# A graph layer's front part: B alone beside the comparisons, A + x behind the counts, and the first 24 rows by searches for the eight largest

## The chip, the cores and the metric

The kernel runs on one core of one Trainium2 chip. The metric is device time of one execution in microseconds (us). The engines are PE (TensorE), DVE (VectorE), ACT (ScalarE), POOL (GpSimd) and SP (SyncE, which issues most DMAs here). Each engine runs its instructions in the order in which the program gives them; PE's clock is granted between half and full speed.

## The reference

x has 6250 rows of 128 numbers; src and dst are 206,250 edges, sorted by dst, each node with a loop of its own.

```python
h = jnp.maximum(_layernorm(x, axis=-1), 0.0)
x_i = h[dst]
x_j = h[src]
feat = jnp.concatenate([x_i, x_j - x_i], axis=-1)
msg = feat @ W.T + b
out = jax.ops.segment_max(msg, dst, num_segments=x.shape[0])
x = x + jnp.where(jnp.isfinite(out), out, 0.0)
```

With W = [W1 W2], msg = A[dst] + B[src], where A = h (W1 - W2)^T + b and B = h W2^T. A[dst] is the same for all edges of one dst, so the output is x + A + the maximum of B[src] over a node's edges.

## The kernel before, in words

Each of 128 partitions takes a window of 1792 edges (WIN) that covers its 49 nodes. The stages, in order of time:

1. **Front (0 to 25.6 us).** The windows are found and gathered (src into swin, dst into pk), masks and tables are made, and the statistics of the first tenth of x.
2. **Comparisons (25.6 to 88).** For 41 lags, `shift` (L530, DVE) compares each edge's node with the one so many places ahead of it, and PE counts the matches into PSUM (`dup`, L519): an edge whose (dst, src block) already had an edge is not handled by the matmuls and goes on the list. Between the lags stand the *linear steps*, three for each k of 25 pairs of 125 rows: `turn` (transposes of h, L421, copy hT L422), `product` (bias L430, two 256-column products L433, copies of B: Bp L437 and a staging copy L438) and `remainder` (negI x Bp L446, copies L448 and L449). They are issued by `ln(n)`; 16 k's are done here, the rest later. B goes to HBM as Bt, A as XA (L455, on SP), and POOL adds x to XA in HBM by five accumulating DMAs (`add_x`, L441).
3. **List (88 to 155).** The sign of the counts (L591, ACT), a running sum over it (L610, the scan) that says how far each kept edge moves, and then 11 compaction passes (`pass_`, L633 and L634, DVE), of 1, 2, 4 ... places. After pass 4, `early` (L643 to L656) finds the first 24 entries of each list, and the first three groups of gathers are issued. PE meanwhile transposes the windows (`turned`, L666) and receives `tick`s: a small memset on DVE (L504) that a matmul waits for (L505), and eight matmuls whose result is not used (`keep_on`, L499). Behind the passes come the list's indices (ridx), the run ends, several checks whose sums go into badc, rows of Sel (`make_sel`, L256), and Sel's last two rows by DMA (L741, SP).
4. **Main loop (155 to 700).** 13 tiles x 25 pairs: one-hot matmuls (L903), ACT (L904), two products with Bp (L981), maximum into acc on DVE (L985, L987). Beside it goes the *stream* of 420 rows of listed edges: POOL gathers row k of all partitions (`gather`, L87) from Bt into the ring X, which holds six groups of eight rows; DVE takes a running maximum (L157, `stream_step`); SP writes each finished group to M (L164). A group's place is gathered into again once its write to M is over. `more_rows` fixes at which pair which gather and which step stands.
5. **End (700 to 767).** The 49 R gathers fetch each node's last row from M (L87, R<-M), then maximum, + XA, and the output.

The tiles of stages 2 and 3 lie in pools that are given back before stage 4. OHQ, the first tile of stage 4 that DVE sets (L885), lies in their memory.

X serves twice: until the linear steps have read x, its columns hold x (`xs`). acc, big and T are also used as temporary memory in the front part.

Of the kernel before, what the change touches and what calls it, by code (L numbers as in the profile page):

```python
# [8 lines left out]
F32 = mybir.dt.float32  # L9
F32R = mybir.dt.float32r  # L10
F16 = mybir.dt.float16
# [42 lines left out]
def gnn_kernel(tc, x, src, dst, W, b, out):  # L54
# [17 lines left out]
    EP = 5  # L72
    EW = 3 * U
    SETS = (WIN - EW - (1 << EP)) // (2 << EP) + 1
    assert EW + (1 << EP) <= 2 << EP and 16 < SETS <= 32 and WIN % (2 << EP) == 0
# [17 lines left out]
    with ExitStack() as ctx:  # L93
# [13 lines left out]
        with ExitStack() as body:  # L107
# [58 lines left out]
            with ExitStack() as pre:  # L166
# [45 lines left out]
                wmask = pool.tile([P, Q], F16, name="wmask")  # L212
# [8 lines left out]
                spare = acc[:1, 4 * GQ * C:]  # L221
# [38 lines left out]
                make_sel(0, 30)  # L260
                warm = pool.tile([P, 1], F32, name="warm")
# [57 lines left out]
                hs = [pool.tile([L, 2, C], F32, name=f"hs{i}") for i in range(2)]  # L319
                hT = [pool.tile([P, 2, P], F32, name=f"hT{i}") for i in range(2)]  # L320
# [22 lines left out]
                iota(pads, [[2, OV]], 0, 0)  # L343
# [27 lines left out]

                fl = pool.tile([P, 2 * NBLK], F32, name="fl")
                fin_ = big[:, :2 * C]
# [32 lines left out]
                bs = spare[:, 512:512 + 3 * P - 1]  # L406
# [4 lines left out]
                stage = acc[:L, :4 * GQ * C].rearrange("l (g q c) -> l g q c", g=4, c=C)  # L411

                def scaled(k):
                    for j in range(2):
                        q = 2 * k + j
                        A_.activation(hs[k % 2][:, j], xs[:, q], AF.Relu, scale=rstd[:, q:q + 1], bias=nmr[:, q:q + 1])  # L416

                def turn(k):
                    pt = ps_t.tile([P, 2, P], F32, name="pt")
                    for j in range(2):  # L420
                        T_.transpose(pt[:, j, :L], hs[k % 2][:, j], ident[:L, :L])  # L421
                    A_.copy(hT[k % 2][:, :, :L], pt[:, :, :L])  # L422

                def where(k):
                    g, o = divmod(2 * k, GQ)
                    return g % 2, o

                def product(k):
                    pm = steps[k]["pm"] = ps_m.tile([P, 2, 2 * C], F32, name="pm")
                    T_.matmul(pm[:L, :, C:], bsel, brow[:, C:].rearrange("k (o c) -> k o c", o=1).to_broadcast([P, 2, C]),  # L430
                              start=True, stop=False, skip_group_check=True)
                    for j in range(2):
                        T_.matmul(pm[:L, j], hT[k % 2][:, j, :L], wT, start=False, stop=j == 1, skip_group_check=True)  # L433
                    if k + 1 < NP_:
                        scaled(k + 1)
                    g, o = where(k)
                    A_.copy(Bp[:L, 0, 2 * k:2 * k + 2], pm[:L, :, :C])  # L437
                    A_.copy(stage[:, g, o:o + 2], pm[:L, :, :C])  # L438

                def add_x(q0):  # L440
                    G_.dma_start(out=XA_l[:, q0:q0 + GQ], in_=x_l[:, q0:q0 + GQ], accum_op=ALU.add)  # L441

                def remainder(k):
                    pm = steps[k].pop("pm")
                    g, o = where(k)
# [3 lines left out]
                    A_.copy(Bp[:L, 1, 2 * k:2 * k + 2], pm[:L, :, :C])  # L449
                    q0 = 2 * k - o  # L450
                    o0 = GQ - 4 if q0 + GQ == Q and o + 2 == GQ else 0
                    if o + 2 == GQ or q0 + GQ == Q and o + 2 == GQ - 4:
                        for to, j in ((Bt_l, g), (XA_l, 2 + g)):
                            for p0, p1 in PARTS:
                                S_.dma_start(to[p0:p1, q0 + o0:q0 + o + 2], stage[p0:p1, j, o0:o + 2])  # L455
                        if q0 + GQ < Q:
                            add_x(q0)

                micro = [lambda: turn(0)]
                for k in range(NP_):  # L460
                    micro.append(lambda k=k: product(k))
                    if k + 1 < NP_:
                        micro.append(lambda k=k: turn(k + 1))
                    micro.append(lambda k=k: remainder(k))

                def ln(n):
                    for _ in range(min(n, len(micro))):
                        micro.pop(0)()

# [9 lines left out]
                A_.activation(s16, sq, AF.Identity, bias=nthr)  # L479
                V.tensor_scalar(l16, sq, 1.0 / Q, (1 - Q) * 0.5 / Q, op0=ALU.mult, op1=ALU.add)  # L480
# [64 lines left out]
                def mine():  # L545
                    V.tensor_tensor(own, dlc, s16, ALU.is_equal)

                    def mm():
                        for c0 in range(0, WIN, 512):
# [9 lines left out]
                among[15] += [lambda: V.scalar_tensor_tensor(dwin, dlc, float(1 << DB), big, op0=ALU.mult, op1=ALU.add)]  # L559
                among[4] += [sel_rows]  # L560
                among[7] += [lambda: A_.activation(big, sq, AF.Copy, scale=float(1 << PB))]
# [7 lines left out]
                for i in range(SH):  # L569
                    among[i].append(lambda i=i: ln(2 if i % 5 == 4 else 1))  # L570
# [5 lines left out]
                flush(0)  # L576

# [8 lines left out]
                val = s16.bitcast(BF16)  # L586
                less = junk[0]
                spread_begin()
# [4 lines left out]
                make_sel(30, 40)  # L593
                finite(w_sb, 2 * C, P, 18)
                for v, op, o in ((VMAX, ALU.is_lt, badc[:L, 16:17]), (-VMAX, ALU.is_gt, badc[:L, 17:18])):
                    V.tensor_scalar(fin_[:L, :Q], mv[:, :, 1], v, None, op0=op, op1=ALU.add, accum_out=o)
                    V.tensor_scalar(o, o, -1.0, float(Q), op0=ALU.mult, op1=ALU.add)

# [10 lines left out]
                V.tensor_copy(u[:, :1], offs[:, :1])  # L609
                V.tensor_tensor_scan(u[:, 1:1 + WIN], sgn[:, :WIN], ones[:, :1].to_broadcast([P, WIN]), offs[:, :1],  # L610
                                     op0=ALU.add, op1=ALU.add)
                V.tensor_scalar(offs[:, 1:], offs[:, :1], -1.0, 2.0 * OV, op0=ALU.mult, op1=ALU.add)
                V.tensor_scalar(pk[:, :OV], pads, offs[:, 1:], 0.0, op0=ALU.subtract, op1=ALU.max)
                ln(2)
                p = ps_m.tile([P, 512], F32, name="pm")
                T_.matmul(p[:P - 1, :1], ident[:, 1:], offs[:, :1], start=True, stop=True)
                V.tensor_scalar(rlim[:P - 1], p[:P - 1, :1], -0.5, float(OV), op0=ALU.mult, op1=ALU.add)
                del p
                V.tensor_scalar_mul(over_, offs[:, 1:], 0.5)
                ln(6)  # L620
# [16 lines left out]

                def early():

                    s2 = 2 << EP  # L640
                    blocks = pk[:, OV:].rearrange("p (m r) -> p m r", r=s2)
                    F, FM = (swin[:, j * 32 * EW:(j + 1) * 32 * EW].rearrange("p (m w) -> p m w", w=EW) for j in range(2))
                    V.memset(mend_i, 0)  # L643
                    gather(mend, M[:P, :], mend_i[:, 0:1])
                    V.tensor_scalar(F[:, :SETS], blocks[:, :SETS, :EW], 0, None, op0=ALU.bitwise_or)
                    src_ = blocks[:, :SETS, s2 // 2:s2 // 2 + EW]
                    V.tensor_scalar(FM[:, :SETS], src_, 2 << EP, None, op0=ALU.bitwise_and)
                    V.copy_predicated(F[:, :SETS], FM[:, :SETS], src_)
                    d = 1
                    while d < SETS:  # L650
                        n = len(range(0, SETS - d, 2 * d))
                        f, m = (t.rearrange("p (a b) w -> p a b w", b=2 * d) for t in (F, FM))
                        V.tensor_scalar(m[:, :n, 0], f[:, :n, d], 4 * d << EP, None, op0=ALU.bitwise_and)
                        V.copy_predicated(f[:, :n, 0], m[:, :n, 0], f[:, :n, d])
                        d *= 2
                    V.tensor_scalar(ridx[:, :EW], F[:, 0], PB, (1 << DB - PB) - 1, op0=ALU.logical_shift_right,  # L656
                                    op1=ALU.bitwise_and)
                    for _ in range(EW // U):
                        gather_group()
                    V.scalar_tensor_tensor(val, dup, 0.0, vm, op0=ALU.is_equal, op1=ALU.mult)  # L660
# [21 lines left out]
                for i in range(EP):  # L682
                    rest[i].append(lambda i=i: ln(4 if i < EP - 1 else len(micro)))
# [6 lines left out]
                for i in (5, 6, 7, 8, 9, 10):  # L690
                    rest[i].append(lambda: tick(8))
# [5 lines left out]
                for i in range(11):  # L697
                    if i == EP:
                        early()
# [3 lines left out]
                add_x(Q - GQ)  # L703
# [8 lines left out]
                moved = u[:, :OV]  # L712
# [7 lines left out]
                for _ in range(GB - EW // U):  # L720
                    gather_group()
                sdl = u[:, OV:GR + OV]
# [16 lines left out]
                make_sel(40, Q)  # L739
# [8 lines left out]
                found()  # L748
                apart()
                finite(bsrc[:1], C, 1, 20)  # L750
# [347 lines left out]
```

## Time and profile before

| what | value |
|---|---|
| time, median of 3 runs (lowest, highest) | 769.29 us (769.13, 771.18) |
| the profiled execution's own time, and its span | 769.23 us, 767.5 us |
| mean granted clock of PE | 0.948 |
| busy: PE, DVE, ACT, POOL | 634.3, 721.8, 481.6, 505.3 us |
| X gathers on POOL | 420, 440.6 us |
| DVE idle in 700 to 768, for X gathers and R gathers | 6.8 us, 5.2 us |

A row of the timeline has the start, the duration, engine, line and operation, then what it writes and reads; in brackets stands the engine's idle time before it, and what ended it. PE's matmuls overlap in its pipe, so their cost is read from one start to the next. A POOL row of a gather is the writing of its descriptors; the transfer follows.

### The profile page before, as it was taken

To read this page: it belongs to the slowest core of one execution; us is meant where nothing else is said; L and a number is where in the kernel's file an instruction comes from. 1 tells how busy PE (TensorE), PEld (TensorE's weight loads), DVE (VectorE), ACT (ScalarE), POOL (GpSimd) and SP (SyncE) were. 2 spreads that over 40 slices of the span, in tenths; PEclk is the share of its full clock that TensorE was granted. 3 is DMA by queue.
4 is the path that set the end of the run, shared out by engine and by line. 5 is a ranking of instruction groups with operands and counts; after the bars stand their busy time and mean duration, and the time that the engine had idled before them with its cause. 6 is when DMAs were issued, how large, how long until landed. Compare 5 with 4: busy or idle time off the path is not lost.

```text
span 767.5 us, 11957 instructions
## 1 busy us (share of the span) xinstructions
PE 634.3 (83%) x3636; PEld 462.9 (60%) x3643; DVE 721.8 (94%) x1306; ACT 481.6 (63%) x1034; POOL 505.3 (66%) x522
## 2 busy tenths in 40 slices
PE   0699873568999898899989899999989899997871
PEld 0356542456667676666757667766757576775660
DVE  8999899979899999999999999999999999998584
ACT  3476681235789999565666767666666667676420
POOL 4000005877777777777777777777777777777774
PEclk9999996859999999999999999999999999999695
DMA  6533542143143433334333343334333343433494
GB/s 196 135 80 97 126 124 62 49 107 107 53 116 104 119 104 86 111 104 116 108 111 91 97 116 107 115 107 116 102 91 107 103 116 104 114 107 106 134 235 149
DMA packets 83699, 85.05 MB, mean 111 GB/s; under 512 B 9996, under 2 KB 71554, under 8 KB 83372
## 3 DMA queue, kind: packets, MB, share of 16 engines
q1 hardware_dynamic: 66951, 47.36, 21.7%
q0 software_dynamic: 16080, 35.93, 17.5%
q10 hardware_dynamic: 596, 0.92, 0.4%
q8 instruction: 30, 0.49, 0.3%
q14 instruction: 42, 0.34, 0.1%
HBM read 46.76 MB, written 40.47 MB: 114 GB/s over the span
## 4 chain that ended last, share of the span: by engine, by line
DVE 29%; PE 21%; issue 15%; DMA 5%; ACT 4%; POOL 2%; DVEq 0%; POOLq 0%
DVE acc L987 18%; PE ps L981 12%; DVE X L157 7%; PE z L903 5%; PE pv L835 4%; DMA X<-Bt,ridx 3%; ACT oh L904 2%; DMA R<-M,last_e 2%; ACT counted L994 2%; DVE OHQ L798 2%; POOL R L87 1%; POOL X L87 1%; DVE OHD L802 1%; DVE R L1019 1%; DVE acc L985 1%
## 5 line engine op out<-in xcount | busy, mean ns | idle before, releaser
L87 POOL DMA_INDIRECT X<-Bt,ridx x420 | 440.6, 1049 | 132.1 <-issue 40.2
L904 ACT ACTIVATE oh<-z 126x490 fp32r<-126x490 f32 (+1 forms) x650 | 340.4, 586 | 165.9 <-PE z L903 164.4
L981 PE MATMUL ps<-oh,Bp 126*128 126x490 f32 (+1 forms) x1300 | 393.3, 425 | 41.3 <-DVE acc L987 40.2
L987 DVE TENSOR_TENSOR acc<-acc,ps 128x980 f32<-128x980 f32 (+1 forms) x312 | 358.8, 1150 | 10.9 <-PE ps L981 8.1
L981 PEld LDWEIGHTS ps<-oh,Bp 126*128 126x128 f32 x1300 | 239.9, 193 | 137.6 <-DVE acc L987 92.3
L903 PE MATMUL z<-Vb,Sel 128*126 128x490 f16 (+1 forms) x650 | 196.1, 377 | 12.2 <-ACT oh L904 9.3
L157 DVE SCALAR_TENSOR_TENSOR X<-X,slim 128x128 f32<-128x128 f32 x419 | 143.5, 342 | 7.6 <-DMA X<-Bt,ridx 3.6
L903 PEld LDWEIGHTS <-Sel 128*126 128x126 f16 x650 | 87.0, 142 | 32.2 <-issue 3.9
L835 PEld LDWEIGHTS <-OHQ 128*128 128x128 bf16 x910 | 62.6, 162 | 16.3 <-issue 15.4
L835 PE MATMUL pv<-OHD,OHQ 128*128 128x28 bf16 (+1 forms) x896 | 67.2, 228 | 3.2 <-DVE OHD L805 3.1
L441 POOL DMA_DIRECT2D XA<-in_x x5 | 4.5, 902 | 89.6 <-DMA XA<-acc 89.6
L798 DVE TENSOR_TENSOR OHQ<-T,IQ 128x1092 bf16<-128x1092 bf16 (+5 forms) x104 | 61.4, 598 | 0.0
L87 POOL DMA_INDIRECT R<-M,last_e x49 | 49.6, 1012 | 16.4 <-issue 11.6
L994 ACT ACTIVATE counted<-lane_dl,nbias 128x556 bf16<-128x556 int32 x50 | 42.7, 853 | 0.1
L519 PE MATMUL dup<-T,identb 128*128 128x512 bf16 (+1 forms) x164 | 39.3, 364 | 3.7 <-DVE T L530 3.5
L433 PE MATMUL pm<-wT,hT 128*125 128x256 f32 x100 | 26.8, 392 | 0.3 <-ACT hT L422 0.3
L519 PEld LDWEIGHTS <-identb 128*128 128x128 bf16 x168 | 15.9, 101 | 17.2 <-issue 5.6
L634 DVE COPY_PREDICATED pk<-big,pk 128x1927 int32<-128x1927 int32 (+12 forms) x13 | 22.9, 1761 | 0.4
L416 ACT ACTIVATE hs<-X,nmr,rstd 125x128 f32<-125x128 f32 x50 | 22.1, 498 | 1.7 <-DVE nmr L314 1.7
L530 DVE TENSOR_TENSOR T<-KA,KB 128x1792 bf16<-128x1792 int16 x21 | 21.6, 1082 | 1.0 <-PE dup L519 1.0
L530 DVE TENSOR_TENSOR T<-KA 128x1792 bf16<-128x1792 int16 x20 | 20.8, 1077 | 0.1
L421 PE MATMUL pt<-ident,hs 125*128 125x125 f32 x50 | 12.6, 303 | 10.0 <-ACT hs L416 9.0
(271 smaller groups left out, 448.3 us busy)
## 6 DMA issues: line engine op xcount, KB each, us to landing
M<-X SPq DMA_DIRECT2D x52, 512.0 KB
X<-Bt,ridx POOLq DMA_INDIRECT x420
XA<-in_x POOLq DMA_DIRECT2D x5, 625.0 KB
ownb<-Bt SPq DMA_DIRECT2D x12, 245.0 KB
X<-in_x SPq DMA_DIRECT2D x5, 560.0 KB
Bt<-acc SPq DMA_DIRECT2D x4, 560.0 KB
XA<-acc SPq DMA_DIRECT2D x4, 560.0 KB
out_x<-R SPq DMA_DIRECT2D x8, 224.0 KB
```

The lines of the kernel that those rows point to most:

```text
L87: G_.indirect_dma_start(out=o, out_offset=None, in_=table, in_offset=bass.IndirectOffsetOnAxis(ap=idx, axis=0))
L157: V.scalar_tensor_tensor(G[:, j], state["prev"], slim[:, k:k + 1], G[:, j], op0=ALU.min, op1=ALU.max)
L433: T_.matmul(pm[:L, j], hT[k % 2][:, j, :L], wT, start=False, stop=j == 1, skip_group_check=True)
L519: T_.matmul(dup[:, c0:c1], w, e[:, c0:c1], start=first, stop=last)
L530: V.tensor_tensor(e, KA[:, 64:], i1, ALU.is_equal)
L798: V.tensor_tensor(OHQ[:, :nl, a:z], over(TQ, z - a), iq, ALU.is_equal)
L835: T_.matmul(o, w, m, start=False, stop=True, skip_group_check=True)
L903: T_.matmul(z[:L + 1, :n], Sel[:, i + j], Vb[t % 2][:, :n], start=True, stop=True)
L904: A_.activation(oh[:, :n], z[:L + 1, :n], AF.Relu)
L981: T_.matmul(ps[:, j, :n], Bp[:, e, i + j], oh[j][:, :n], start=e == 0, stop=e == 1)
L987: V.tensor_tensor(a, a, ps[:, :, :n], ALU.max)
L994: A_.activation(counted.bitcast(BF16)[:, :NS], lane_dl, AF.Sign, scale=2.0, bias=nbias[:, c:c + 1], accum_out=ends[:, c:c + 1])
```

## The change

- The steps beside the comparisons compute B alone: `turn` and a `product` of two 128-column matmuls; its second copy goes to a staging area in big, and hT of all k stays (in acc). All 50 steps stand between the lags.
- A + x is a *second* piece for each k, `second(k)`: bias, two 256-column products, a matmul of the unit matrix with x, and negI x Bp; then two copies on ACT and XA's two DMAs on SP. `add_x` on POOL is gone. One second step stands behind the sign, three ahead of the scan, two each in passes 0 to 7 (16), and the last five behind the list, ahead of the sixth group of gathers.
- `early` is gone. `lead(g)` finds the first 24 entries, eight at a time, with DVE's MAX over the first 896 edges of an order number that POOL prepares, and MATCH_REPLACE takes out what was found. lead(0) stands behind the scan, lead(1) behind pass 1, lead(2) behind pass 3, and the first group of gathers behind each.
- The checks `found`, `apart` and `finite(bsrc)` stand under the wait for the sign instead of behind the list; Sel's rows 30 to 49 are made on ACT, four rows a pass; the ticks in the passes are gone, the two behind the list stay. `dwin` and its scaled src move ahead, the list's pads go to ACT, and a check for windows of which 896 edges hold too few entries is new.

The core of the diff:

```diff
+                def lead(g):
+                    V.max(top8, order)
+                    r = ridx[:, g * U:g * U + U]
+                    V.tensor_scalar(r, top8, 0.0, None, op0=ALU.max)
+                    V.tensor_scalar(r, r, PLACE - 1, None, op0=ALU.bitwise_and)
+                    gather_group()
+                    if g + 1 < EW // U:
+                        V.match_replace(order, top8, order, 0.0)
...
+                def second(k):
+                    pm = ps_m.tile([P, 2, 2 * C], F32, name="pm")
+                    pa = pm[:L, :, C:]
+                    T_.matmul(pa, bsel, brow[:, C:].rearrange("k (o c) -> k o c", o=1).to_broadcast([P, 2, C]),
                               start=True, stop=False, skip_group_check=True)
                     for j in range(2):
-                        T_.matmul(pm[:L, j], hT[k % 2][:, j, :L], wT, start=False, stop=j == 1, skip_group_check=True)
...
+                        T_.matmul(pm[:L, j], hT[:, 2 * k + j], wT, start=False, stop=False, skip_group_check=True)
+                    T_.matmul(pa, ident[:L, :L], xs[:, 2 * k:2 * k + 2], start=False, stop=True, skip_group_check=True)
                     T_.matmul(pm[:L, :, :C], negI[:L, :L], Bp[:L, 0, 2 * k:2 * k + 2], start=False, stop=True,
                               skip_group_check=True)
-                    A_.copy(stage[:, 2 + g, o:o + 2], pm[:L, :, C:])
+                    t = hs[k % 4]
+                    A_.copy(t, pa)
                     A_.copy(Bp[:L, 1, 2 * k:2 * k + 2], pm[:L, :, :C])
...
+                    for p0, p1 in PARTS:
+                        S_.dma_start(XA_l[p0:p1, 2 * k:2 * k + 2], t[p0:p1])
...
-                    among[i].append(lambda i=i: ln(2 if i % 5 == 4 else 1))
+                    among[i].append(lambda i=i: ln(2 if i % 4 == 3 else 1))
...
+                V.tensor_tensor(ahead, twice, u[:, :EX], ALU.subtract)
+                V.scalar_tensor_tensor(order, ahead, 0.0, order_, op0=ALU.is_ge, op1=ALU.mult)
...
+                rest[0] += [lambda: ln2(2), lambda: gather(mend, M[:P, :], mend_i[:, 0:1])]
+                rest[1] += [lambda: ln2(2), lambda: lead(1)]
+                rest[2] += [lambda: ln2(2)]
+                rest[3] += [lambda: ln2(2), lambda: lead(2),
+                            lambda: V.scalar_tensor_tensor(val, dup, 0.0, vm, op0=ALU.is_equal, op1=ALU.mult)]
+                for i in range(4, 8):
+                    rest[i].append(lambda: ln2(2))
...
-                for i in (5, 6, 7, 8, 9, 10):
-                    rest[i].append(lambda: tick(8))
...
-                for _ in range(GB - EW // U):
+                for i in range(GB - EW // U):
+                    if i == GB - EW // U - 1:
+                        ln2(len(micro2))
                     gather_group()
```

DVE's instructions around the scan, before. swin holds the scan's sums, pk the list, big the mask of a pass:

```order
L617 TENSOR_SCALAR rlim<-pm 127x1
L619 TENSOR_SCALAR over__97<-offs 128x1
L621 TENSOR_TENSOR pk<-pk,swin 128x1792
L633 TENSOR_SCALAR big<-pk 128x1927
L634 COPY_PREDICATED pk<-big,pk 128x1927
```

The same place in the changed kernel, from the scan to the second pass; T_82 holds ahead and KB the order numbers:

```order
L650 SCALAR_TENSOR_TENSOR swin<-T_82,offs,ones 128x1792
L652 CAST swin<-offs 128x1
L654 TENSOR_TENSOR T_82<-T_82,swin 128x896
L655 SCALAR_TENSOR_TENSOR KB<-T_82,KA 128x896
L613 MAX top_980<-KB 128x8
L615 TENSOR_SCALAR ridx<-top_980 128x8
L616 TENSOR_SCALAR ridx<-ridx 128x8
L619 MATCH_REPLACE KB<-top_980,KB 128x896
L659 TENSOR_SCALAR rlim<-pm 127x1
L661 MEMSET mend_i 128x1
L662 TENSOR_TENSOR pk<-pk,swin 128x1792
L674 TENSOR_SCALAR big<-pk 128x1927
```

Six instructions (L654 to L619) now stand between the scan and the first pass, two of them searches over 896 elements; ridx, which the gathers wait for, is written before the passes and no longer between the fifth and the sixth.

PE behind the list, in the changed kernel; L519 is the tick's matmul, L513 the first of eight keep-on matmuls, and L455 to L460 are one second step (the first of five is shown), L759 the heads matmul:

```order
L519 MATMUL dup<-tick,identb 128x1
...
L513 MATMUL dup<-zero,identb 128x256
L455 MATMUL pm<-brow,bsel 125x2x128
L458 MATMUL pm<-wT,acc 125x256 x2
L459 MATMUL pm<-X,ident 125x2x128
L460 MATMUL pm<-Bp,negI 125x2x128
...
L759 MATMUL pm<-heads,ident 127x1
```

Before, the heads matmul (L736) came right behind the eight keep-on matmuls of the tick; now five second steps, of five matmul instructions each, stand between them.

SP's queue at the same place, in the changed kernel; hs_239 to hs_242 are the buffers t of the second steps:

```order
L717 DMA first<-pk 15x136
L466 DMA XA<-hs_239 112x256
L466 DMA XA<-hs_239 13x256
...
L466 DMA XA<-hs_239 112x256
L466 DMA XA<-hs_239 13x256
L763 DMA Sel<-mrow_161 1x50x126 x2
```

Before, Sel's DMAs (L741) followed the DMAs of first directly; now the ten XA DMAs of the last five second steps are ahead of them in the queue.

More of the change, by code (lines that the diff above doesn't have):

```diff
@@ L260, in gnn_kernel, with sel_act @@
                 make_sel(0, 30)
+                def sel_act(q0, q1):
+                    for q in range(q0, q1):
+                        A_.activation(Sel[:, q], wrow, AF.Identity, scale=wmask[:, q:q + 1])
+                srcf = Sel.rearrange("k q m -> k (q m)")[:, 35 * (L + 1):].bitcast(F32)[:, :EX]
                 warm = pool.tile([P, 1], F32, name="warm")
@@ L318, in gnn_kernel @@
                 negI = pool.tile([P, P], F32R, name="negI")
-                hs = [pool.tile([L, 2, C], F32, name=f"hs{i}") for i in range(2)]
-                hT = [pool.tile([P, 2, P], F32, name=f"hT{i}") for i in range(2)]
+                hs = [pool.tile([L, 2, C], F32, name=f"hs{i}") for i in range(4)]
+                hT = acc[:, :Q * L].rearrange("c (q l) -> c q l", l=L)
                 V.tensor_scalar_mul(negI, ident, -1.0)
@@ L370, in gnn_kernel @@
                 S_.dma_start(at(Bt, N * C, [[C, NPAD - N], [1, C]]), zero[:NPAD - N, :2 * C].bitcast(F32))
+                front = pool.tile([P, EW], BF16, name="front")
+                G_.memset(front, 0.0)
+                G_.affine_select(out=front, in_=front, compare_op=ALU.not_equal, fill=256.0, base=1 - P, pattern=[[0, EW]],
+                                 channel_multiplier=1)
                 fl = pool.tile([P, 2 * NBLK], F32, name="fl")
-                fin_ = big[:, :2 * C]
+                fin_ = KB.bitcast(F32)[:, :2 * C]
                 def finite(t, n_, m_, c):
@@ L420, in turn @@
                     for j in range(2):
[L421 to L426, printed above, removed]
-                def product(k):
-                    pm = steps[k]["pm"] = ps_m.tile([P, 2, 2 * C], F32, name="pm")
-                    T_.matmul(pm[:L, :, C:], bsel, brow[:, C:].rearrange("k (o c) -> k o c", o=1).to_broadcast([P, 2, C]),
+                        T_.transpose(pt[:, j, :L], hs[k % 4][:, j], ident[:L, :L])
@@ L451, in remainder @@
[L451 to L457, printed above, removed]
+                    for p0, p1 in PARTS:
+                        S_.dma_start(XA_l[p0:p1, 2 * k:2 * k + 2], t[p0:p1])
@@ L463, in gnn_kernel @@
                         micro.append(lambda k=k: turn(k + 1))
-                    micro.append(lambda k=k: remainder(k))
+                micro2 = [lambda k=k: second(k) for k in range(NP_)]
                 def ln(n):
@@ L468, in ln, with ln2 @@
                         micro.pop(0)()
+                def ln2(n):
+                    for _ in range(min(n, len(micro2))):
+                        micro2.pop(0)()
                 vm = pool.tile([P, WIN], BF16, name="vm")
@@ L548, in mm @@
                     def mm():
+                        T_.matmul(dup[:, :EW], identb, front, start=False, stop=False)
                         for c0 in range(0, WIN, 512):
@@ L576, in gnn_kernel @@
                 flush(0)
+                ln(len(micro))
                 u = swin
@@ L636, in pass_ @@
                             done()
[L638 to L660, printed above, removed]
                 def turned(s, t, h):
@@ L702, in gnn_kernel @@
                         f()
-                add_x(Q - GQ)
+                V.tensor_scalar(over_, offs[:, :1], -0.5, float(OV), op0=ALU.mult, op1=ALU.add)
+                V.tensor_scalar(badc[:, 11:12], u[:, EX - 1:EX], 2.0 * (EX - 1 - EW), None, op0=ALU.is_gt)
                 V.tensor_tensor(nres, listed[:, :1], listed[:, 1:], ALU.add)
```

92 lines of the change are left out of this document (52 added, 40 removed).

## The prediction

> **What bounds the kernel now.** I read the busy time by stretch first, then the waits of the last stretch, then the groups.
>
> ```profile
> 60.00:80.00 20.00, 19.61 (x107) 12.64 (x108) 19.93 (x41) 14.79 (x46) 0.85 (x1) 1.00 0.39 97
> 100.00:148.00 48.00, 27.16 (x285) 19.35 (x285) 46.35 (x68) 21.69 (x60) 23.09 (x16) 0.86 0.34 89
> 400.00:700.00 300.00, 276.52 (x1568) 204.05 (x1568) 299.09 (x500) 198.67 (x386) 232.05 (x224) 1.00 0.38 107
> ```
>
> After the stretch and its length stand the busy times of PE, PEld, DVE, ACT and POOL, then PE's granted clock. The reader is to see three regimes. In the comparisons (60 to 80) PE and DVE are both full. In the list stage (100 to 148) DVE alone is full. In the long middle (400 to 700) DVE is full, and POOL is too, although it reads 232 of 300: each gather is followed by a gap that no other work fills.
>
> ```profile
> 217.17 0.95 POOL L87 DMA_INDIRECT X<-Bt,ridx  x1 [0.30 <-issue]
> 218.42 0.94 POOL L87 DMA_INDIRECT X<-Bt,ridx  x1 [0.30 <-DVE acc L991]
> ...
> 719.90 0.94 POOL L87 DMA_INDIRECT R<-M,last_e  x1 [0.30 <-issue]
> ```
>
> One gather starts every 1.25 us (217.17 to 218.42). From the first one on, POOL has this chain and hardly another wait, to the R gathers at 719.90. Who is late at the end is in the waits of DVE from 700 on:
>
> ```profile
> DVE X L157 <- DMA X<-Bt,ridx: 3.6, 2, 2.3
> DVE X L157 <- issue: 3.2, 2, 1.8
> ```
>
> DVE waits 3.6 + 3.2 = 6.8 us there for gathered rows. So the end is the gather chain's end, and DVE has 6.8 us of room behind it. After the last X gather come the R gathers and a fixed tail. **The time therefore moves as the gather chain moves**, as long as DVE does not slip more than 6.8 us against it. The profiled execution took 769.23 us (span 767.5), the median is 769.29, so a shift can be added to either.
>
> **Comparisons.** One of PE's groups in 25.6 to 88 counts the linear steps done there before, 16:
>
> ```profile
> L430 PE MATMUL pm<-brow,bsel 128*125 128x256 f32 x16 | 6.0, 375 | 0.0
> ```
>
> Records overlap in the pipe, so I price by starts, in one step of before:
>
> ```profile
> 94.70 0.38 PE L430 MATMUL pm<-brow,bsel 128*125 128x256 f32 x1 [0.74 <-ACT Bp L449]
> 94.92 1.02 PE L433 MATMUL pm<-wT,hT 128*125 128x256 f32 x4
> 95.79 0.38 PE L421 MATMUL pt<-ident,hs 125*128 125x125 f32 x2
> ```
>
> The bias product holds PE for 0.22, the two 256-column products for 0.87, and a 256-column negI product for 0.22 like the bias. A step with its transposes (0.25) was 1.56, and 16 of them lay here: 25 us. Now 25 steps of half a product and the transposes, 0.44 + 0.25, come to 17. PE is relieved of 8 us, but DVE is equally full here, so only PE's backlog at the end can shrink.
>
> ```profile
> 86.10 1.46 DVE L256 TENSOR_TENSOR Sel<-wmask,wrow 128x1260 f16<-128x1260 f16 x1
> 88.63 1.01 ACT L591 ACTIVATE T<-dup,pos_h 128x896 bf16<-128x896 f32 x1 [0.93 <-issue]
> ...
> 149.77 0.14 DVE L381 TENSOR_TENSOR fl<-sums 128x1 f32<-128x1 f32 x1
> ...
> 151.98 0.14 DVE L378 TENSOR_SCALAR badc<-badc 1x1 f32<-1x1 f32 x1
> ```
>
> The last comparison is over when the Sel rows start at 86.10, and the sign of the counts starts at 88.63; the backlog is 2.5 and one comparison's counting of some 0.9 must stay. I take -1.2; ends: -3.4 (the whole backlog, and some 0.9 more where DVE waited for PE's counts) and +2 (the copies on ACT or the B writes become late). The checks moved under the wait for the sign lie beside ACT's 2 us of signs and cost nothing there; without that cover they are the 2.3 us that they took from 149.77 to 152.1.
>
> **List stage, on DVE alone.** New are ahead, order, three MAX and two MATCH_REPLACE, seven operations on 896 four-byte elements, and six tiny ones.
>
> ```profile
> 92.64 3.94 DVE L610 TENSOR_TENSOR_SCAN swin<-T,offs,ones 128x1792 int32<-128x1792 bf16 x1
> 97.00 2.02 DVE L621 TENSOR_TENSOR pk<-pk,swin 128x1792 int32<-128x1792 int32 x1
> 99.04 1.16 DVE L633 TENSOR_SCALAR big<-pk 128x1927 int32<-128x1927 int32 x1
> ...
> 116.97 0.06 DVE L643 MEMSET mend_i<- 128x1 int32 x1
> ...
> 122.01 0.18 DVE L656 TENSOR_SCALAR ridx<-swin 128x24 int32<-128x24 int32 x1
> 122.10 2.02 DVE L660 SCALAR_TENSOR_TENSOR s<-dup,vm 128x1792 bf16<-128x1792 f32 x1
> ```
>
> No row shows MAX or MATCH_REPLACE. At the rate of the plain 1792-element rows (2.02) 896 elements take 1.05; at that of the fast one 0.54; at the scan's, 1.97. I take 1.05, the rate of L621 and L660: 7 x 1.05 = 7.35 (ends 3.8 and 13.8). Six tiny ones at 0.18: 1.1. The old search goes, 122.10 - 116.97 = 5.13, and small steps (pads and offsets now on ACT, six tick memsets, against a bound and a new check): -0.5. Sum +2.8. All of it is on DVE's path, for no other engine is late in this stage. The list's end, marked by the tick memset of 144.04, comes at 144.04 - 1.2 + 2.8 = 145.64.
>
> **From the list's end to the main loop.** Before:
>
> ```profile
> 144.04 0.06 DVE L504 MEMSET tick<- 128x1 bf16 x1
> ...
> 155.20 0.96 DVE L885 MEMSET OHQ<- 128x588 uint32 x2 [0.49 <-ACT KB L753]
> ```
>
> OHQ, the first one-hot tile, was set 11.16 us behind the tick, released by an ACT sum of DVE's order check. DVE's work in between loses Sel's last rows (1.46 for as many, at 86.10) and the checks (2.3), so DVE would be ready sooner. But OHQ takes the memory of the front part and so waits for all of it: now also for the last five second steps on PE, their copies, their XA writes, and Sel's two writes behind those in SP's queue. On PE the five stand behind the tick and its eight keep-on matmuls; the heads matmul stands behind them, and DVE's cast of mend_i waits for that (behind the cast stands OHQ's memset, which is later anyway). This chain is priced with PE's clock:
>
> ```profile
> 127.53 0.16 PE L505 MATMUL dup<-tick,identb 128*128 128x1 bf16 x1 [10.84 <-DVE tick L504]
> 127.56 1.87 PE L499 MATMUL dup<-zero,identb 128*128 128x256 bf16 x8
> 132.04 1.03 PE L499 MATMUL dup<-zero,identb 128*128 128x256 bf16 x8
> 120.00:128.00 8.00, 0.47 (x4) 0.34 (x4) 7.66 (x14) 0.00 (x0) 4.44 (x3) 0.50 0.08 18
> 128.00:132.00 4.00, 3.33 (x37) 2.53 (x37) 3.94 (x4) 0.97 (x2) 3.68 (x2) 0.60 0.08 20
> ```
>
> After 10.84 idle us the clock was 0.50; a mean of 0.60 over 128 to 132 puts the rise at 131.2, 3.7 us after PE resumed. With the ticks of the passes gone, PE has nothing to do from the last transposes (19 steps of 1.74 from about 92 on and 12 groups of transposes of about 1 us, which wait for no pass: an estimate of 137 to 139) to 145.7: it starts cold. A second step at full clock: 0.22 bias + 0.87 + 0.43 for x (half of 0.87) + 0.22 = 1.74, at half clock some 3.4. So 0.1 + 1.87 for tick and keep-on, then 1.7 us of cold clock for half a step, then 4.5 x 1.74 = 7.8: the steps end 11.5 us behind the tick.
>
> ```profile
> 85.93 0.37 ACT L437 CAST Bp<-pm 125x256 fp32r<-125x256 f32 x1 [0.34 <-PE pm L433]
> ...
> 109.64 0.83 SPq L455 DMA_DIRECT2D XA<-acc  x2
> 149.69 1.53 SPq L741 DMA_DIRECT2D Sel<-mrow  x2
> ```
>
> The copy and its start add 0.6 (it takes 0.37), the XA issues 0.8, the first of Sel's two issues 0.8, and the second lands some 2.6 later (an estimate: a landing in the chain of waits is 2.2 to 3.7 long, in the rows below). In all 11.5 + 0.6 + 0.8 + 0.8 + 2.6 = 16.3 instead of 11.16. OHQ comes at 145.64 + 16.3 = 161.9, **the main loop 6.7 us later** than from 155.2.
>
> The Trainium skill, "TensorE: Matmul & The Clock Gate", Part 1, "What's actually happening", has the clock judged in a free-running window of 3413 ns and raised after one busy window. By that rule the rise comes 3.4 to 6.8 us after the resumption, an estimate from that page; the trace agrees with its low end (3.7), and the sum by it would be up to 1.5 us longer, 775.
>
> **What the gathers make of it.** The first X gather moves from 122.96 to about 100, and the fifth accumulating DMA of x leaves POOL. Under the passes a gather is slow:
>
> ```profile
> 126.29 2.45 POOL L87 DMA_INDIRECT X<-Bt,ridx  x1 [0.30 <-issue]
> 129.06 3.08 POOL L87 DMA_INDIRECT X<-Bt,ridx  x1 [0.32 <-issue]
> ```
>
> With 2.75 to 3.4 us from one to the next, 23 us give 7 or 8 rows, worth some 10 us at 1.25. But the ring X has six groups of eight rows, and group 9 goes where group 3 was until group 3's write to M has landed:
>
> ```profile
> 221.77 9.83 SPq L164 DMA_DIRECT2D M<-X  x2
> 227.62 1.05 POOL L87 DMA_INDIRECT X<-Bt,ridx  x1 [0.31 <-DVE acc L987]
> ...
> 170.63 2.21 DMA X<-Bt,ridx
> ...
> 327.85 3.69 DMA X<-Bt,ridx
> ```
>
> Group 3's write is issued at 221.77 and group 9's first gather starts at 227.62: 5.85 us, of which 2.2 to 3.7 are the landing. Room: 2.2 to 3.6; I take 2.4, landing 3.4. The writes follow DVE's steps and come 6.7 later, so group 9 starts 6.7 - 2.4 = 4.3 later than before, whatever lead there was. From there POOL runs without a gap as before and never makes it up: the end is +4.3. DVE slips 6.7 - 4.3 = 2.4 against it, less than its room of 6.8.
>
> Sum: 769.23 + 4.3 = **773.5**. Ends of the parts: list 3.8 to 13.8 for 7.35 (-3.5, +6.5), comparisons (-2.2, +3.2), chain to OHQ (-1.8 warm, +1.6), room of the ring (+0.2, -1.2). They seldom add up; as independent ones they give 770 to 778.
>
> **Rivals.** (A, the other side) PE stays warm. Then keep-on takes 1.03 and the steps 8.7, OHQ comes 0.1 + 1.03 + 8.7 + 0.6 + 0.8 + 0.8 + 2.6 = 14.6 behind the tick, and the wait of the first pair goes as well:
>
> ```profile
> 152.00:172.00 20.00, 11.69 (x96) 9.22 (x95) 15.29 (x37) 6.11 (x11) 15.93 (x15) 0.50 0.45 105
> 171.75 1.18 DVE L985 TENSOR_TENSOR acc<-ps,acc 128x980 f32<-128x980 f32 x1 [3.74 <-PE ps L981]
> ```
>
> PE ran the start of the loop at 0.50, and DVE waited 3.74 for its first sums. Loop later by 1.6 + 14.6 - 11.16 - 3.74 = 1.3; less the room of 2.4 it is -1.1: **768**. It decides from the point where the loop slips less than the 2.4 us of room. For it: five dense steps end just before the loop. Against it: some 5 us between them and the first one-hot, in a stretch where before the clock stayed at 0.50 beside scattered matmuls. Where MAX and its kin also run at the fast rate, it is 764.5. Chance 0.15.
>
> (B) The gathers' lead is not stopped by the ring, because some group's room is larger than I read. Then DVE's end sets the time: its 6.8 us of waits go, its loop comes 6.7 later, so its last step stays at about 721; 22 of the 49 R gathers need the last row, and 721 + 3.7 + 22 x 1.25 + 8 of tail + 1.7 is **762**. Against it: the two rows of group 3 and 9. The lead itself is uncertain: the Trainium skill, "SBUF — State Buffer", "SBUF: two separate sides", says GpSimd cannot write a gather's descriptors until DVE gives up the shared port. The two slow gathers agree (2.45 and 3.08 instead of 0.94); were it not so, the lead would be 22 us by that page, and the ring would take it just the same. Chance 0.08.
>
> (C) Slower still: the new searches run at the scan's rate (+6.5), or the comparisons lose by ACT's copies and B's writes. 3 to 6.5 more than the forecast: **777 to 780**, middle 778. For it: MAX must keep eight values per element, and no row shows what that costs. Against it: one element per cycle is what the plain rows show. Chance 0.17.
>
> (D) The steps do not hold OHQ at all (they are done in time, or the early gathers do nothing): OHQ at 155.2 + 1.6 - 3, then the room is not used up and it is about 768 as in A. I count it into A.
>
> **How the numbers follow.** Forecast 0.60, with its own range of 770 to 777. A measurement of this kernel tells 0.3% (2.3 us) from no change, so the bounds are 766.9 and 771.6. Faster: B 0.08 and a third of A 0.05, 0.13. Same: the rest of A 0.10 and the low part of the forecast 0.10, 0.20. Slower: 0.50 of the forecast and C, 0.67. The range leaves out B and the outer parts of A and C: 766 to 779.
>
> **What would show it.** Right: the tick memset near 145.6; seven list operations of about 1.05; PE's clock near 0.5 when the five steps start and a pause of DVE's cast for PE; OHQ's memset near 162 and released by a DMA; group 9's first gather near 232 although the first one starts near 100; waits of DVE for gathers after 700 of some 4.4. Wrong: a clock of 1.0 through the five steps and first pairs (A), R gathers that start before 719.90 (B), searches of 2 us each (C).

## The result, and the profile after

The changed kernel takes 777.47 us (median of 5 runs, 775.7 to 780.53) against 769.29 before (5 runs, 769.02 to 771.18): 8.2 us more, a ratio of 1.0106 with a 95% interval of 1.0079 to 1.0134. Its profiled execution is the median one, 777.47 us with a span of 775.8 (before 767.5). Ten of the twelve runs below fell on chips where the engines stood still for tens of microseconds behind 150 us, whichever the kernel (before took 1042 to 1107 us there): they are called disturbed below, and of them only the stretch up to 150 us is read, and single waits where the text says so.

Where the list ends and the main loop starts, DVE's timeline of the changed kernel:

```profile
93.90 3.95 DVE L650 TENSOR_TENSOR_SCAN swin<-T,offs,ones 128x1792 int32<-128x1792 bf16 x1
...
148.63 0.06 DVE L518 MEMSET tick<- 128x1 bf16 x1
...
159.49 0.16 DVE L783 CAST mend_i<-pm 127x1 int32<-127x1 f32 x1 [3.98 <-PE pm L759]
164.44 0.96 DVE L904 MEMSET OHQ<- 128x588 uint32 x2 [4.79 <-DMA Sel<-mrow]
```

The reader is to see two new waits, 3.98 us for the heads matmul behind the five second steps and 4.79 us for Sel's DMA. The scan starts 1.26 us later than before (92.64), the tick 4.59 (144.04), OHQ 9.24 (155.20).

PE's timeline over the same place, with its clock in two stretches of the windows:

```profile
148.76 0.16 PE L519 MATMUL dup<-tick,identb 128*128 128x1 bf16 x1 [13.85 <-DVE tick L518]
148.78 1.87 PE L513 MATMUL dup<-zero,identb 128*128 128x256 bf16 x8
150.30 0.56 PE L455 MATMUL pm<-brow,bsel 128*125 128x256 f32 x1
...
153.04 0.28 PE L455 MATMUL pm<-brow,bsel 128*125 128x256 f32 x1
...
154.02 0.60 PE L459 MATMUL pm<-X,ident 125*125 125x256 f32 x2
154.26 0.47 PE L460 MATMUL pm<-Bp,negI 125*125 125x256 f32 x1
154.57 0.28 PE L455 MATMUL pm<-brow,bsel 128*125 128x256 f32 x1
...
159.18 0.28 PE L759 MATMUL pm<-heads,ident 128*127 128x1 f32 x2
148.00:152.00 4.00, 3.24 (x14) 2.53 (x14) 3.70 (x14) 0.00 (x0) 3.00 (x4) 0.50 0.19 49
152.00:156.00 4.00, 4.00 (x21) 3.51 (x20) 3.31 (x20) 1.29 (x4) 3.39 (x3) 0.93 0.29 81
```

PE was idle for 13.85 us and starts at half clock (0.50); the first second step takes 2.74 (150.30 to 153.04), the next 1.53. A mean of 0.93 over 152 to 156 puts the clock's rise at 152.6, 3.8 us after PE resumed. SP's queue shows what follows:

```profile
153.68 6.89 SPq L466 DMA_DIRECT2D XA<-hs  x10
160.66 1.56 SPq L763 DMA_DIRECT2D Sel<-mrow  x2
```

Sel's writes are issued once the ten XA writes are, and OHQ starts 3.8 us behind the first of them. Then POOL and SP, at the last two groups of the ring that wait:

```profile
102.51 0.99 POOL L87 DMA_INDIRECT X<-Bt,ridx  x1 [9.30 <-issue]
...
223.44 1.21 POOL L87 DMA_INDIRECT X<-Bt,ridx  x1 [13.44 <-DVE X L157]
...
234.93 0.94 POOL L87 DMA_INDIRECT X<-Bt,ridx  x1 [1.20 <-DVE X L157]
...
725.58 0.95 POOL L87 DMA_INDIRECT X<-Bt,ridx  x1 [0.30 <-DVE acc L1006]
...
765.91 0.94 POOL L87 DMA_INDIRECT R<-M,last_e  x1 [0.31 <-issue]
230.80 19.95 SPq L164 DMA_DIRECT2D M<-X  x3
```

The first gather is 20.5 us earlier than before, and POOL then stands still for 2.88 us at group 6, 13.44 at group 8 and 1.20 at group 9. Group 9 starts at 234.93, 4.1 us behind the issue of group 3's write to M (230.80); groups 6 and 8 start 4.1 and 4.2 behind the writes of groups 0 and 2. The rows name DVE's step, which had long been done. Against before (227.62) group 9 is 7.3 us late, the last X gather 6.9 (718.65), the last R gather 7.4 (758.55), and 0.9 comes on top behind it. DVE's waits after 705:

```profile
DVE X L157 <- DMA X<-Bt,ridx: 1.2, 1, 1.2
DVE X L157 <- issue: 1.1, 1, 1.1
```

They are 2.3 instead of 6.8: the loop slipped against the gathers, and some room is left.

### The profile page after: what moved, and what is told of

It reads as the page before. It is cut to its first block, busy times and chain, and to the rows that moved or that the text cites. A ratio compares the mean times of both kernels' runs of the same rounds, so it can differ in the third digit from the quotient of the medians.

```text
span 775.8 us, 12309 instructions
## 1 busy us (share of the span) xinstructions
PE 643.6 (83%) x3740; PEld 474.4 (61%) x3740; DVE 723.5 (93%) x1298; ACT 488.4 (63%) x1056; POOL 513.5 (66%) x523
## 4 chain that ended last, share of the span: by engine, by line
DVE 33%; PE 17%; issue 16%; ACT 8%; DMA 7%; POOL 4%; DVEq 0%; POOLq 0%; ACTq 0%
DVE acc L1006 16%; PE ps L1000 10%; DVE X L157 6%; DMA X<-Bt,ridx 5%; ACT oh L923 4%; PE z L922 4%; ACT counted L1013 3%; DVE pk L675 3%; PE pv L854 3%; POOL R L87 3%; DMA R<-M,last_e 2%; POOL X L87 2%; DVE big L674 1%; DVE OHQ L817 1%; DVE acc L1004 1%
## 5 line engine op out<-in xcount | busy, mean ns | idle before, releaser
L87 POOL DMA_INDIRECT X<-Bt,ridx x420 | 448.2, 1067 | 157.8 <-issue 67.7
L1000 PEld LDWEIGHTS ps<-oh,Bp 126*128 126x128 f32 x1300 | 237.1, 191 | 136.4 <-DVE acc L1006 89.8
L157 DVE SCALAR_TENSOR_TENSOR X<-X,slim 128x128 f32<-128x128 f32 x419 | 145.9, 348 | 3.2 <-DMA X<-Bt,ridx 1.2
L463 ACT COPY hs<-pm 125x256 f32<-125x256 f32 x25 | 9.3, 374 | 36.8 <-issue 20.6
L458 PE MATMUL pm<-wT,acc 128*125 128x256 f32 x100 | 26.5, 389 | 0.0
```

The lines of the kernel that those rows point to most:

```text
L87: G_.indirect_dma_start(out=o, out_offset=None, in_=table, in_offset=bass.IndirectOffsetOnAxis(ap=idx, axis=0))
L157: V.scalar_tensor_tensor(G[:, j], state["prev"], slim[:, k:k + 1], G[:, j], op0=ALU.min, op1=ALU.max)
L1000: T_.matmul(ps[:, j, :n], Bp[:, e, i + j], oh[j][:, :n], start=e == 0, stop=e == 1)
```

## The experiments

**Five second steps ahead of the list's end.** Nothing else differs from the changed kernel.

```diff
+                rest[8].append(lambda: ln2(2))
+                rest[9].append(lambda: ln2(3))
```

> The changed kernel with its last five second steps in passes 8 and 9 (two and three) instead of behind the list; nothing else differs. Ring theory (the loop's start is set by the five steps, their XA and Sel writes; the ring hands the loop's delay, less some 2 us of room, to the gathers and so to the end): DVE itself is done with the list's end at 155.5 and ACT's sum at about 156, so OHQ is set near 156.5 instead of 164.44, PE works through the steps before the tick, and the time falls by 7 to 8 us to about 769.5 to 770.5. Rival, list theory (the longer searches on DVE and the later scan make the time; the five steps are hidden beside the end of the list): no more than 3 us less, 774.5 or above.

> The kernel of the first run once more, since there the stretch behind 150 us was disturbed by stalls of 24 us and more on PE. Ring theory: OHQ near 156.5 instead of 164.44, the time 7 to 8 us less than the changed kernel's, 769.5 to 770.5. List theory: no more than 3 us less, 774.5 or above.

These two runs were disturbed, at equal ticks (148.60 and 148.91). The third was not:

> The kernel with the five second steps in passes 8 and 9, one look, for an execution that is not disturbed behind 150 us. Ring theory: OHQ near 156.5, 769.5 to 770.5. List theory: 774.5 or above.

It took 770.03 us, before 768.71 on the same chip (one execution each). DVE, ACT and SP at the loop's start, and POOL at groups 8 and 9:

```profile
148.74 0.06 DVE L518 MEMSET tick<- 128x1 bf16 x1
...
156.24 0.96 DVE L906 MEMSET OHQ<- 128x588 uint32 x2 [0.56 <-ACT KB L774]
```

```profile
146.57 1.52 SPq L765 DMA_DIRECT2D Sel<-mrow  x2
```

```profile
215.29 1.21 POOL L87 DMA_INDIRECT X<-Bt,ridx  x1 [8.00 <-DVE X L157]
...
226.75 0.94 POOL L87 DMA_INDIRECT X<-Bt,ridx  x1 [1.18 <-DVE X L157]
```

With the tick where it was, OHQ is 8.2 us earlier (164.44 to 156.24) and released by ACT's order check as before the change; group 9 is 8.2 earlier (234.93 to 226.75), and the time is 7.4 lower than the changed kernel's median (its lowest is 775.7). That is the ring theory's number, in one execution, and the list theory's 774.5 is excluded. The rest of the change, searches included, leaves the time about where it was: the lead of 20 us at the first gather ends in a wait of 8.00 us. Against the trace of before the last R gather is 0.2 earlier (758.34), and the stretch behind it 1.0 longer. The edit moves the steps on PE, their copies and their XA writes at once; Sel's writes alone, ahead of the XA writes in SP's queue, were not tried.

**A ring of eight groups.** Two groups more lie in R's first 16 columns, which are fetched last.

```diff
+GT = 8
-                s = i % GB * U * C
-                return X[:, s:s + U * C].rearrange("p (u c) -> p u c", c=C)
+                s = i % GT * U * C
+                o = more[0][:, s - GB * U * C:s + U * C - GB * U * C] if s >= GB * U * C else X[:, s:s + U * C]
+                return o.rearrange("p (u c) -> p u c", c=C)
...
-                        if state["gathered"] < NG and state["ran"] > (state["gathered"] - GB + 1) * U:
+                        if state["gathered"] < NG and state["ran"] > (state["gathered"] - GT + 1) * U:
```

> The changed kernel with a ring of eight groups: the two added groups lie in R, whose columns 0 to 15 are fetched last; the loop's start stays as late as it is. Ring theory: group 9 no longer waits for group 3's write, the lead of the early gathers (first one at 102.5) reaches the end of the stream, DVE's waits for gathers after 700 go, and the end follows DVE's last step (about 726) plus a landing and 22 R gathers: about 768, at most 771. Rival (the gathers are late for another reason: slow ones beside the passes, or DVE's pace): no change, 776 to 779.

> The ring of eight groups once more, for the same reason. Ring theory: the loop starts as late as in the changed kernel (OHQ near 164.4), but no gather of groups 6 to 9 waits for a write to M, DVE's waits for gathers after 700 go, and the time is about 768, at most 771. Rival (the gathers are late for another reason): no change, 776 to 779.

> The changed kernel with a ring of eight groups, for undisturbed executions. Ring theory: OHQ as late as in the changed kernel (164.4), but group 9 starts near 218 instead of 234.9, DVE's waits for gathers after 700 go, and the end follows DVE's last step (about 726): 768, at most 771. Rival (the gathers are late for another reason): 776 to 779.

All three runs of it alone were disturbed (ticks 148.55, 149.28 and 148.82; 148.63 in the changed kernel). In all three POOL goes on into group 9 without a wait (0.30 us), where the six disturbed runs with six groups have one of 1.18 to 1.20; but the loop came 29 to 31 us later there, and POOL stood still for 16 us at group 8 until group 0's write was over. So the expected time is left undecided; so is that of ring and moved steps together, in a run that was disturbed too:

> Ring of eight groups and the five second steps in passes 8 and 9 together. Ring theory: OHQ near 156.5 and the gathers' lead of about 10 us kept, so DVE's last step comes near 716 and bounds the end, with 22 R gathers behind it: 757 to 760, under both kernels. If the lead cannot be kept because POOL or DVE is at its limit already in the long middle: 768 to 770, as with the steps alone.

**Ring, moved steps, and one linear step fewer between the lags.** The third edit:

```diff
-                    among[i].append(lambda i=i: ln(2 if i % 4 == 3 else 1))
+                    among[i].append(lambda i=i: ln(2 if i % 5 == 4 else 1))
```

> Ring of eight groups, five second steps in passes 8 and 9, and one linear step fewer between the lags, so that the last product of B comes behind the counts. In the front part, whatever the rest does: if the last products between the last lags hold the counts up (PE waits there for ACT's copies of hT), the sign starts 0.9 us earlier than in the run with the five steps moved (near 88.4) and the tick near 147.8; if DVE's comparisons alone set it, nothing changes (89.3 and 148.7). In the whole, ring theory: OHQ near 155.4, no gather of groups 6 to 9 waits for a write to M, DVE's last step near 715: 756 to 760, under both kernels. If POOL or DVE is at its limit anyway: 768 to 770.

Undisturbed, 764.49 us (5 runs, 762.66 to 767.46; the profiled one took 765.6) against 770.45 before on the same chip (8 runs): ratio 0.9922, interval 0.9895 to 0.995. It is 6.0 us under before, and 13.0 under the changed kernel's median, which was not measured beside it; more was expected. First the front part, ACT's timeline:

```profile
90.37 0.37 ACT L449 CAST Bp<-pm 125x256 fp32r<-125x256 f32 x1 [1.58 <-PE pm L444]
90.64 0.38 ACT L450 COPY big<-pm 125x256 f32<-125x256 f32 x1
90.90 1.02 ACT L628 ACTIVATE T<-dup,pos_h 128x896 bf16<-128x896 f32 x1
```

The third edit was a miss: the last product now comes behind the counts on PE, but its two copies stand ahead of the sign in ACT's queue, and the sign starts at 90.90 instead of 0.9 us earlier than 89.3. OHQ came at 157.83. The test gives the products no support and does not refute them: the counts were over at 89.90, 2.7 us behind DVE's last comparison (87.16), against 2.5 in the changed kernel.

The ring did what was expected of it. POOL at groups 8 and 9 (L88 is the gather there), the end of the chain, SP at group 3, DVE's last steps, and the landing of one R gather:

```profile
207.94 0.94 POOL L88 DMA_INDIRECT R<-Bt,ridx  x1 [0.31 <-DMA R<-Bt,ridx]
209.19 0.95 POOL L88 DMA_INDIRECT X<-Bt,ridx  x1 [0.30 <-DMA R<-Bt,ridx]
...
220.00 1.63 POOL L88 DMA_INDIRECT X<-Bt,ridx  x1 [0.31 <-DVE acc L1013]
...
705.32 0.94 POOL L88 DMA_INDIRECT X<-Bt,ridx  x1 [0.30 <-DVE acc L1013]
706.57 0.94 POOL L88 DMA_INDIRECT R<-M,last_e  x1 [0.30 <-issue]
...
728.48 0.94 POOL L88 DMA_INDIRECT R<-M,last_e  x1 [0.70 <-DVE acc L1013]
732.32 0.94 POOL L88 DMA_INDIRECT R<-M,last_e  x1 [2.90 <-DMA R<-M,last_e]
...
752.88 0.94 POOL L88 DMA_INDIRECT R<-M,last_e  x1 [0.30 <-issue]
224.25 10.97 SPq L168 DMA_DIRECT2D M<-X  x2
...
716.52 0.73 DVE L161 SCALAR_TENSOR_TENSOR X<-X,slim 128x128 f32<-128x128 f32 x2
726.83 13.48 DMA R<-M,last_e
```

Group 9 starts at 220.00, ahead of group 3's write (224.25), which its six-group forerunners had to wait for. The last X gather is 12.0 us earlier than with the moved steps alone (705.3 against 717.3), although the loop starts 1.6 later, and DVE waits for no gather any more. Of the 12 us only 5.4 reach the last R gather (752.9 against 758.3): 34 R gathers are left then, not 30, since fewer of them had been issued among the X gathers (5.0 us at 1.25), and they wait 1.6 us more, 2.90 at the longest (732.32). So POOL bounds the end again, not DVE's last step. That step came at 716.9, near the 715 expected, and the 22 R gathers that were counted behind it and its landing were left then (721.83 to 752.88). But their starts spread over 31.05 us, where 21 times 1.25 is 26.25: POOL waited 4.9 us in all for R gathers to land (3.0 in before), and the one issued at 726.83 landed 13.48 us later. The profile has the DMA engines' mean busy share at 0.90 to 1.10 in 720 to 740; that this made the landings long is read from these figures, not tested. These waits, a loop 2.4 us later than the 155.4 expected, and a stretch behind the last R gather of 11.0 instead of 8.95 in before are why 756 to 760 was missed.

**The old search.** `early` stands again between passes 4 and 5, and `lead`, its two preparing operations, POOL's order numbers and the new check are left out.

```diff
-                V.tensor_tensor(ahead, twice, u[:, :EX], ALU.subtract)
-                V.scalar_tensor_tensor(order, ahead, 0.0, order_, op0=ALU.is_ge, op1=ALU.mult)
...
-                lead(0)
...
+                    if i == EP:
+                        early()
                     pass_(i, hand_over)
```

> The changed kernel with the old search for the first 24 rows between passes 4 and 5 in the place of the three searches for eight largest (and without POOL's order numbers and the check that goes with them); first gather near 123 instead of 102.5. Ring theory: the early gathers' lead is worth nothing, DVE's list is 3 to 4 us shorter, OHQ comes 3 to 4 us earlier, and the time falls by as much: about 773.5 to 774.5. Rival, lead theory (the early gathers still pay part of the delay): the time stays at 777.5 or rises.

> The kernel with the old search once more, one look, since its first run was disturbed behind 150 us (its tick came at 144.9 there, 3.7 us earlier than in the changed kernel). Ring theory: OHQ 3 to 4 us earlier than 164.4, the time 773.5 to 774.5. Lead theory (the early gathers pay part of the delay): 777.5 or more.

> The changed kernel with the old search, for undisturbed executions. Ring theory: tick at 144.9, OHQ near 160.7, and the time falls as much as OHQ comes earlier, 3.7 us: 773.5 to 774.5, although its first gather comes 21 us later. Lead theory: 777.5 or more.

All three runs were disturbed. Up to 150 us, the last of them on DVE:

```profile
91.45 0.35 DVE L634 TENSOR_SCALAR flow<-level,listed 128x128 f32<-128x128 f32 x1 [0.79 <-ACT T L623]
...
144.69 0.06 DVE L520 MEMSET tick<- 128x1 bf16 x1
```

The tick is 3.9 us earlier than in the changed kernel (148.63; the other two runs have 144.93 and 144.70), the price of the new searches against the old one: 0.6 ahead of the scan (93.26 against 93.90) and 3.3 from the scan to the tick. With the old search that stretch is 51.43 us, as before (51.40), so the rest of the change, the second steps beside the passes included, is even there. What the old search would do to the whole time was not measured.

**The ticks of the passes put back.**

```diff
+                for i in (5, 6, 7, 8, 9, 10):
+                    rest[i].append(lambda: tick(8))
```

> The changed kernel with the six ticks in passes 5 to 10 put back, so that PE does not fall idle for 13.9 us before the tick. Clock as part of the price: keep-on takes 1.0 instead of 1.9 and the first second step 1.5 instead of 2.7, less 0.4 for the tick memsets on DVE: heads matmul near 157.5 instead of 159.2, OHQ 1.5 us earlier, about 776. Rival (the chain's length is set by the copies and DMAs, not by PE's clock): unchanged or 0.4 us more, 777.5 to 778.

The tick came at 148.98, 0.35 later than in the changed kernel, as six memsets should cost; the five steps fell into the disturbed stretch, so what a warm PE would give in time was not measured. On PE alone they then took 7.76 us without a gap (184.92 to 192.68), against 8.88 in the changed kernel (150.30 to 159.18).

## Why the prediction was right, and where its sizes were off

The direction, the mechanism and the range held: 777.5 in 766 to 779. But the likeliest time was 773.5, and 777.5 lies just outside the forecast's own 770 to 777: of the 3.9 us too few, 2.5 are the loop's start, 0.5 the ring's room and 0.9 the stretch behind the last R gather. By its steps:

- **Comparisons: -1.2 predicted, +0.6 at the sign, +1.26 at the scan.** This is the term that was most mis-sized. PE was relieved (busy for 54.3 us of 25.6 to 86, before 57.1: by 2.8, not 8) but did not get ahead. Its waits in 26 to 89, its rows at the end of the stage, and DVE's row behind its last comparison:

```profile
PE pm L440 <- ACT acc L435: 2.3, 5, 0.5
```

```profile
86.18 0.70 PE L440 MATMUL pm<-wT,acc 128*125 128x128 f32 x4 [0.46 <-ACT acc L435]
86.72 2.43 PE L533 MATMUL dup<-T,identb 128*128 128x512 bf16 x12
86.55 0.41 DVE L386 TENSOR_SCALAR_CACHE_REDUCE KB<-w_sb 128x256 f32<-128x256 f32 x1
```

DVE was through 0.45 later than before (86.55 against 86.10), and the sign began at 89.24 (88.63 before): the backlog is 2.7 us and not the 1.3 that the prediction left of 2.5. Twelve counting matmuls stood ahead of the sign then, four for each of the three buffers of comparisons, and DVE had waited for PE's counts shortly before, 0.44 and 0.60 us at 80 to 84, as in before (0.42 and 0.56). So PE was still the one waited for. The linear steps now run up to the last lag, and a product waits for ACT's copy of hT ahead of the counts in PE's order; that these waits (2.3 us in all) keep the backlog up is an inference from the rows, which the run meant to test it leaves open. The sign does not wait for POOL's order numbers: with the old search, without them, it came at 89.27 to 89.54. The other 0.65 us was not foreseen at all:

```profile
91.36 1.07 DVE L638 TENSOR_SCALAR flow<-level,listed 128x128 f32<-128x128 f32 x1 [0.79 <-ACT T L624]
90.47 1.88 POOL L627 TENSOR_TENSOR KA<-KA,T 128x896 f32<-128x896 f32 x1 [2.12 <-ACT T L624]
```

The first of DVE's operations behind the sign took 1.07 instead of 0.34 while POOL multiplied its order numbers (90.47 to 92.35); in the run with the old search, where POOL does nothing there, it took 0.35.

- **List: +2.8 predicted, +3.33 measured** (tick minus scan). The unknown operations were priced nearly rightly, at the rate of the plain rows (1.05). DVE's groups in 88 to 160:

```profile
L613 DVE MAX8 top<-KB 128x8 f32<-128x896 f32 x3 | 3.3, 1098 | 0.0
L619 DVE MATCH_REPLACE8 KB<-top,KB 128x896 f32<-128x896 f32 x2 | 2.2, 1077 | 0.0
L619 DVE MATCH_VALUE_LOAD KB<-top,KB 128x8 f32 x2 | 0.2, 85 | 0.0
```

So the searches were not slow, as rival C had it; 7 operations at 1.09 are 0.3 more than counted, the two loads 0.2.

- **Tick to OHQ: 16.3 predicted, 15.8 measured** (164.44 - 148.63), with PE cold as foreseen. The steps ended sooner (10.5 behind the tick, not 11.5): a second step takes 1.53 by its starts and not 1.74, since x's product with the unit matrix costs 0.25 and not 0.43, and the keep-on matmuls take 1.52 (148.78 to 150.30) and not 1.87. Sel's landing took longer (OHQ 3.0 behind the second issue, not 2.6).
- **Loop: +6.7 predicted, +9.2 measured,** the sum of the three.
- **Room of the ring: 2.4 predicted, 1.9 measured** (9.24 - 7.31 at group 9); a group was free 4.1 us behind the issue of its write, not 3.4. The landing had been taken from rows of X gathers; no row of a write to M was behind it. The end of the gathers moved by 7.4, not 4.3.
- **Behind the last R gather: nothing predicted, +0.9 measured.** It lies behind the last sum (L1039 at 768.96, before L1020 at 761.71): from its start to the end of the span are 6.8 us, 5.8 before, and 6.7 and 7.0 in the two other undisturbed runs of kernels with the change. No run explains it.

Of the rivals, A (a warm PE) is refuted by the clock of 0.50 and by the 3.6 us that the first pair still waited:

```profile
180.93 1.18 DVE L1004 TENSOR_TENSOR acc<-ps,acc 128x980 f32<-128x980 f32 x1 [3.61 <-PE ps L1000]
```

C gave the right time (777 to 780). Its first reason, slow searches, is refuted; its second, that the comparisons lose by ACT's copies, is where most of the miss lies, but the copies' part in it is not shown, and of its 3 to 6.5 us the comparisons gave 2.5. B, the lead past the ring, did not happen with six groups, and did in the run with eight: there the lead shortens the time, as far as the R gathers let it. Moving the five steps removes the loop's delay (shown, in one execution); 764.5 is shown for the three edits together, and what the ring alone gives there is not.

## What to carry to other kernels

A step that is put behind the work it does not belong to lengthens whatever waits for the whole stage's memory: look up what the first tile of the next stage waits for, and price the queue (PE, copy, DMA, DMA) to its last link. An early start of a prefetch is worth no more than the ring lets through; read from the group whose place is freed last, before counting a lead as a gain. A relieved engine gives the stage nothing if it is still the one waited for where the stage ends: look there, and not at its mean load.

## What the runs showed of the hardware that was not expected

A small DVE operation (128x128, from SBUF) took 1.07 us instead of 0.34 beside a POOL multiplication of 128x896 four-byte elements that took 1.88; in every run with that POOL operation it took 1.07, without it 0.34 or 0.35. It ended 0.08 or 0.09 us behind the POOL operation in each (92.43 against 92.35 here), so the runs cannot tell a slower operation from one that waits for POOL. MAX8 over 896 elements costs what a plain operation of two inputs over as many costs (1.10 against 1.09).
